# Graph kernel with four layers: the last batch's gate products and layer 3 rows move from GpSimd to VectorE, and the order of all work is planned again

## The chip, the cores and the metric

The kernel runs on one core of a Trainium2 chip. The metric is the device time of one execution in microseconds, taken as the median of several runs. The core has five engines that work side by side, each on its own queue of instructions: TensorE (PE in the profile), VectorE (DVE), ScalarE (ACT), GpSimd (POOL) and SyncE (SP), which here only issues DMAs.

## The reference

There are 16 graphs (batches 0 to 15) of 1024 nodes with 128 features, each with a weighted adjacency matrix of 1024 x 1024 in float32. Four layers follow one another; each takes h = relu(layernorm(x)) and adds its result to x:

```
layer 0, three times:  h = h W + b;  nh = h / |h|;  h = (adj * (nh nh^T)) h      (relu after the first two)
layer 1:  y = relu(((1+eps) h + adj^T h) W1 + b1) W2 + b2, masked by node
layer 2:  softmax(where(adj > 0, tanh(s1_i + s2_j), -1e15)) (h W)
layer 3:  h' = x W^T + b;  e = h' (A + A^T) h'^T;  att = softmax(where(adj > 0, e, 0), axis=1) * adj
          hp = relu(att h')
          i, f, o = sigmoid(gate_k([x, hp]))       (three gates, one number per node each)
          result = o * tanh(sigmoid(i * hp + f * x))
```

In layer 3, x stands for the layer's normalized input. The three gates scale whole rows of 128 features by one number per node. These scalings, and the product with adj in the attention, are what the change moves.

## The kernel before, in words

A batch lies in SBUF as [128 partitions, 8 blocks x 128 features]; node c*128 + p is block c of partition p. The 1024 x 1024 matrices are worked through in eight rows of blocks (index j), each in two halves of 512 columns (HALVES)[...]. Matrices of the form S S^T are symmetric: class Square computes only the blocks on and above the diagonal (L753) and fills in the others by transposing kept blocks (kept by ScalarE at L785, transposed by TensorE at L763). In batches 1 to 13 one quarter of the mirrored blocks goes by VectorE (L775) and a round trip through HBM instead.

Layer 3 (`layer3`) has for each row j: the mask (L1169, VectorE, two halves), the maximum of the row (L1181, VectorE), exp with the row's sum (L1185, ScalarE), the product with adj (L1194, VectorE, two halves), the reciprocal of the sum (L1199) and the scaling of h' by it (L1203, ScalarE), then two accumulating matmuls (`accumulate`, L815). In the last two batches every second row's product with adj is one instruction on GpSimd instead (L1190). After the loop come the eviction of the sums (L615), a small projection psN (L593), its eviction hp (L1216) and `finish`.

`finish(lo, hi)` computes the gates (L1237 VectorE, L1261 ScalarE, L1262 VectorE), z = f * hn on GpSimd (L1265), z = i * hp + z, two Tanh (L1241, L1242), z = o * z + x, and issues the output's DMA on ScalarE's queue (L1272). The two multiply-add steps are in `scaled`. For most batches it is eight VectorE instructions, one for each block of 128 features (L1255). For batches 14 and 15 (`late`) it is one product and one sum on GpSimd (L1248, L1249) for the whole range. Batch 15 calls finish twice, for blocks 0 to 3 and 4 to 7; every other batch calls it once for all eight blocks.

Nothing is issued in the order in which it is written. Every step is recorded as an Op with its engine, an assumed duration and the buffers that it reads and writes. `Plan.order` then plays all of them through once, when the kernel is built: it takes the engine that can start earliest, and among that engine's ready steps the one with the smallest rank. A step's rank is its batch's deadline, less the assumed time of what still hangs on it, less its lead:

```
lead = self.leads.get(o.key + o.edge, self.leads.get(o.key, 0.0))
o.rank = (self.deadline(o.batch) - o.tail - lead, o.seq)
```

Deadlines are 60 apart (PERIOD), the last batch's only LAST behind that of the one before. LEADS is a table of numbers by layer, engine and tile, with own entries for the first two batches (<0, <1) and the last two (>1 for batch 14, >0 for batch 15). POOLS gives the number of buffers of each sort; KINDS gives, by use, the sort, the most that may be held, and the most for a batch that is not the oldest. A larger lead makes a step go earlier. Steps with the flag `port` on VectorE, and all of GpSimd, exclude one another in the plan. The order that comes out is the order of each engine's queue on the chip.

Of the kernel before, what the change touches and what calls it, by code (L numbers as in the profile page):

```python
# [8 lines left out]
F32 = mybir.dt.float32  # L9
# [3 lines left out]
AX = mybir.AxisListType  # L13
# [209 lines left out]
def tile_adj_preln(  # L223
# [66 lines left out]

    R = B * NB
# [22 lines left out]
    eye3 = const.tile([D, E3], F32, name="eye3")  # L314
    load_const(third, b3e[:, 0:D], L3_W_b.partition_broadcast(P))
    for g, (w, v) in enumerate(((L3_ig_w, L3_ig_b), (L3_fg_w, L3_fg_b), (L3_og_w, L3_og_b))):
        at = slice(D + g, D + g + 1)
        load_const(third, w3e[:, at], w[0, 0:D].rearrange("(p o) -> p o", o=1))
        load_const(third, eye3[:, at], w[0, D : 2 * D].rearrange("(p o) -> p o", o=1))
        load_const(third, b3e[:, at], v.partition_broadcast(P))  # L320
    for load_it in first:
        load_it()
# [10 lines left out]
    POOLS = {"adjT": 16, "adjL": 5, "x": 3, "big": 13, "above": 2, "got": 1, "bank": 8, "small": 29, "row": 8, "hbm": 3, "hrow": 2}  # L333
    KINDS = {
        "adjT": ("adjT", 16, 16), "adjL": ("adjL", 5, 5), "x": ("x", 3, 3), "w4": ("big", 10, 6),
        "chunk": ("big", 12, 4), "above": ("above", 2, 1), "got": ("got", 1, 1), "ps": ("bank", 8, 8),
        "acc": ("bank", 8, 8), "small": ("small", 7, 6), "row": ("row", 4, 2), "hbm": ("hbm", 3, 2),
        "hrow": ("hrow", 2, 1),
    }
    PERIOD, LAST, AHEAD, WINDOW = 60.0, 9.0, 2, 0.05  # L340

    LEADS = {
        "0 ACT hT": 10, "0 ACT hn": -27, "0 DVE hn": -7.5, "0 DVE mv": 18.5, "0 DVE nb": -2, "0 DVE st": -7,
        "0 PE ps": 6, "0 POOL rstd": -23, "00 ACT above": -218, "00 ACT hT": 68.5, "00 ACT hTn": -53.5,
        "00 ACT sq": -48, "00 DMA by": 63.5, "00 DMA got": -27.5, "00 DVE above": -233, "00 DVE ew": -9,
        "00 DVE h": -18.5, "00 DVE ss": -111, "00 PE acc0": -166.5, "00 PE ps": -134, "00 PE psP": -26,
        "01 ACT above": 3.5, "01 ACT hT": 55, "01 ACT hTn": -8.5, "01 ACT sq": 54.5, "01 DMA by": -23,
        "01 DMA got": 26, "01 DVE above": 4, "01 DVE ew": 108.5, "01 DVE h": -56, "01 DVE ss": 126.5,
        "01 PE acc0": -136, "01 PE ps": 9, "01 PE psP": -303.5, "02 ACT above": 5, "02 ACT hTn": -115.5,
        "02 ACT sq": 6.5, "02 DMA by": 38, "02 DMA got": -41, "02 DVE above": -10.5, "02 DVE ew": -116,  # L350
        "02 DVE h": -5, "02 DVE ss": -17, "02 DVE x": -78, "02 PE acc0": -116, "02 PE ps": -15, "02 PE psP": 12,
        "02 PE sq": 175, "02 POOL rn": 47.5, "1 ACT g": -36, "1 ACT hn": -48.5, "1 ACT y1": -1.5,
        "1 DMA adjL": -41.5, "1 DVE adjL": -57, "1 DVE hn": -11.5, "1 DVE mv": -94, "1 DVE nb": 152,
        "1 DVE st": -539.5, "1 DVE x": 119.5, "1 PE acc1": -1, "1 PE py": -157, "1 PE py2": -10.5,
        "1 POOL rstd": -12, "2 ACT e2": -4, "2 ACT h": 114.5, "2 ACT hfl": -3.5, "2 ACT hn": -82,
        "2 ACT hnT": -9, "2 DVE alone": 5, "2 DVE e2": 105, "2 DVE h": -2.5, "2 DVE hn": 2.5,
        "2 DVE hrow": -74.5, "2 DVE mv": 11.5, "2 DVE nb": 36.5, "2 DVE rden": 26.5, "2 DVE st": -3,
        "2 DVE x": -11, "2 PE acc2": 5.5, "2 PE p1": 1.5, "2 PE pf": 22, "2 PE ps": 23.5, "2 PE psP": -299.5,
        "2 POOL rstd": 4.5, "3 ACT above": 93, "3 ACT e3": 29, "3 ACT gT": 13.5, "3 ACT gate": -70,
        "3 ACT h3T": -6, "3 ACT hn": 9, "3 ACT hnT": 66.5, "3 ACT hp": -371, "3 ACT hs": -94, "3 ACT z": -137,  # L360
        "3 DMA by": -47.5, "3 DMA got": 34.5, "3 DMA z": -167.5, "3 DVE above": 23.5, "3 DVE e3": -253.5,
        "3 DVE gate": -473.5, "3 DVE h": -119, "3 DVE hn": -0.5, "3 DVE mv": -27.5, "3 DVE nb": 25,
        "3 DVE st": -150, "3 DVE top": -14, "3 DVE z": -942, "3 PE acc3": -134, "3 PE pg": -81, "3 PE ps": 54,
        "3 PE psN": -465.5, "3 PE psP": 3.5, "3 PE sq": 73, "3 POOL rstd": -109.5, "3 POOL z": -13.5,
        "T ACT adjT": -44, "T DMA adjT": 10.5, "T DVE adjT": -411.5, "0 ACT hT <0": -20.5, "0 ACT hT <1": 6,
        "0 ACT hT >0": 6, "0 ACT hT >1": 12, "0 ACT hn <0": -3, "0 ACT hn <1": 49, "0 ACT hn >0": 0,
        "0 ACT hn >1": 31, "0 DVE hn <0": -146.5, "0 DVE hn <1": -18, "0 DVE hn >0": -50, "0 DVE hn >1": 34,
        "0 DVE mv <0": -8.5, "0 DVE mv <1": 29.5, "0 DVE mv >0": 4, "0 DVE mv >1": -11, "0 DVE nb <0": 27,
        "0 DVE nb <1": -61, "0 DVE nb >0": -16.5, "0 DVE nb >1": 51.5, "0 DVE st <1": -11.5, "0 PE ps <0": 25.5,
        "0 PE ps <1": 4, "0 PE ps >0": 9, "0 PE ps >1": 22, "0 POOL rstd <0": 35, "0 POOL rstd <1": 12.5,  # L370
        "0 POOL rstd >0": -77, "0 POOL rstd >1": -19.5, "00 ACT above <0": -4, "00 ACT above <1": -60,
        "00 ACT above >0": -198.5, "00 ACT above >1": -41.5, "00 ACT hT <0": 1.5, "00 ACT hT <1": 11,
        "00 ACT hT >0": 21.5, "00 ACT hT >1": -18, "00 ACT hTn <0": -28.5, "00 ACT hTn <1": 60.5,
        "00 ACT hTn >0": -127, "00 ACT hTn >1": -97.5, "00 ACT params <0": -7.5, "00 ACT sq <0": 223,
        "00 ACT sq <1": 321.5, "00 ACT sq >0": -46, "00 ACT sq >1": 179.5, "00 DMA by <1": 0.5,
        "00 DMA got <1": -76, "00 DMA params <0": 12, "00 DVE above <1": -159, "00 DVE ew <0": 0,
        "00 DVE ew <1": -57.5, "00 DVE ew >0": -155, "00 DVE ew >1": -235.5, "00 DVE h <0": -3,
        "00 DVE h <1": -148.5, "00 DVE h >0": 45, "00 DVE h >1": -2.5, "00 DVE params <0": 60,
        "00 DVE ss <0": 109, "00 DVE ss <1": 12.5, "00 DVE ss >0": -8.5, "00 DVE ss >1": -228.5,
        "00 PE acc0 <0": -64, "00 PE acc0 <1": -216.5, "00 PE acc0 >0": -246, "00 PE acc0 >1": -266.5,  # L380
        "00 PE params <0": 101, "00 PE ps <0": 0, "00 PE ps <1": -36.5, "00 PE ps >0": 39, "00 PE ps >1": -91.5,
        "00 PE psP <0": 20, "00 PE psP <1": -2, "00 PE psP >0": 47, "00 PE psP >1": -187.5, "00 PE sq <1": 51,
        "00 PE sq >0": -4, "00 PE sq >1": 3, "01 ACT above <0": 49.5, "01 ACT above <1": -68.5,
        "01 ACT above >0": -16, "01 ACT above >1": 0, "01 ACT hT <0": 8, "01 ACT hT <1": -76.5,
        "01 ACT hT >0": 21, "01 ACT hT >1": -53.5, "01 ACT hTn <0": 15, "01 ACT hTn <1": -21,
        "01 ACT hTn >0": 10, "01 ACT hTn >1": 0, "01 ACT sq <0": 29, "01 ACT sq <1": 86, "01 ACT sq >0": -54,
        "01 ACT sq >1": 6.5, "01 DMA by <1": 0, "01 DMA got <1": 29, "01 DVE above <1": 0, "01 DVE ew <0": 24,
        "01 DVE ew <1": 57, "01 DVE ew >0": 205.5, "01 DVE ew >1": -87, "01 DVE h <0": -89.5,
        "01 DVE h <1": -30.5, "01 DVE h >0": -5, "01 DVE h >1": 0, "01 DVE ss <0": 29, "01 DVE ss <1": 29.5,
        "01 DVE ss >0": 45, "01 DVE ss >1": -13, "01 PE acc0 <0": 0, "01 PE acc0 <1": -39.5,  # L390
        "01 PE acc0 >0": -2, "01 PE acc0 >1": 3, "01 PE ps <1": 9.5, "01 PE ps >0": 6, "01 PE psP <0": 11,
        "01 PE psP <1": -150.5, "01 PE psP >0": -16.5, "01 PE psP >1": -73, "01 PE sq <0": 67,
        "01 PE sq <1": -4, "01 PE sq >0": 5, "01 PE sq >1": 4.5, "01 POOL rn <0": -3.5, "01 POOL rn <1": -3.5,
        "01 POOL rn >0": -3.5, "01 POOL rn >1": -3.5, "02 ACT above <0": 20, "02 ACT above <1": 23,
        "02 ACT above >0": 30, "02 ACT above >1": -7, "02 ACT hTn <0": -14.5, "02 ACT hTn <1": 48,
        "02 ACT hTn >0": -16, "02 ACT hTn >1": 45.5, "02 ACT sq <0": 37, "02 ACT sq <1": -112,
        "02 ACT sq >0": 0.5, "02 ACT sq >1": 67.5, "02 DMA by <1": 23, "02 DMA got <1": -100,
        "02 DVE above <1": 0, "02 DVE ew <0": -27, "02 DVE ew <1": -155.5, "02 DVE ew >0": -74.5,
        "02 DVE ew >1": -196, "02 DVE h <0": 1.5, "02 DVE h <1": -37, "02 DVE h >0": -20.5,
        "02 DVE h >1": -32.5, "02 DVE ss <0": -12.5, "02 DVE x <0": -108, "02 DVE x <1": -32,  # L400
# [993 lines left out]
```

## Time and profile before

| | us |
|---|---|
| median of three runs | 2461.91 (2461.11 to 2462.0) |
| the profiled execution | 2464.46 |
| span of its profile | 2462.7 |
| TensorE busy | 2397.5 |
| VectorE busy | 2106.1 |
| ScalarE busy | 1291.5 |
| GpSimd busy | 254.5 |
| L1190, eight on GpSimd | 20.1 |
| L1194, 240 half rows on VectorE | 157.2 |
| L1255, 224 multiply-adds on VectorE | 61.1 |

The times of the profile belong to the one profiled execution. Busy time of one engine overlaps with that of others, so the sums say little on their own; what counts is which engine works while TensorE does not. A line of a stretch gives its bounds in us from the start of the span, its length, and for each engine the busy time and, behind the x, the number of instructions that began in it; PEclk is the granted clock of TensorE, DMA the busy share of the DMA engines. A matmul of float32 stands in the trace as two records.

### The profile page before, as it was taken

Reading aid. Unit: us, or ns where it says so; the run is one execution under the profiler, and the core shown is the slowest. Engines: PE = TensorE matmul, PEld = TensorE weight load, DVE = VectorE, ACT = ScalarE, POOL = GpSimd, SP = SyncE. Lnnn points to the kernel's source line nnn. Section 1 sums busy time; section 2 is a strip of 40 time slices with the busy share of each in tenths; the row PEclk is TensorE's granted clock in tenths of the full one; section 3 lists DMA queues with packets and bytes.
Section 4 is the critical chain, followed back from the end, with each engine's and each line's share of the span. In section 5 each row is a group of like instructions: output and inputs, shape, how many; then the busy total and the mean of one; then the engine's idle time right before and its main releaser. Section 6 shows DMA issues by size and latency. Waiting matters only on the chain.

```text
span 2462.7 us, 34845 instructions
## 1 busy us (share of the span) xinstructions
PE 2397.5 (97%) x11946; PEld 1592.9 (65%) x11946; DVE 2106.1 (86%) x5232; ACT 1291.5 (52%) x2404; POOL 254.5 (10%) x155
## 2 busy tenths in 40 slices
PE   6999999999999999999999999999999999999985
PEld 3568576775756657576675766657576675765763
DVE  6758889888998989899898998989899898897585
ACT  4415564735546465464644646465464745656274
POOL 1001010100101101010010101101010010100025
PEclk9999999999999999999999999999999999999998
DMA  8731929658394764928649394774929646072000
GB/s 132 125 103 35 167 56 144 139 89 160 72 159 112 107 142 94 174 67 147 136 82 167 65 164 114 100 145 93 173 73 146 134 86 133 28 96 75 26 1 18
DMA packets 1129473, 263.35 MB, mean 107 GB/s; under 512 B 971856, under 2 KB 1112912, under 8 KB 1129296
## 3 DMA queue, kind: packets, MB, share of 16 engines
q1 hardware_dynamic: 1108368, 251.73, 57.3%
q10 hardware_dynamic: 20928, 9.40, 1.4%
q8 instruction: 94, 1.54, 0.3%
q14 instruction: 83, 0.68, 0.1%
HBM read 198.14 MB, written 62.91 MB: 106 GB/s over the span
## 4 chain that ended last, share of the span: by engine, by line
PE 86%; DVE 5%; DMA 4%; ACT 3%; SPq 1%; POOL 1%; issue 0%; POOLq 0%; DVEq 0%; ACTq 0%
PE acc L815 33%; PE sq L753 17%; PE acc L826 17%; PE psP L593 6%; PE sq L763 4%; PE py L1014 2%; PE py L603 2%; PE ps_hTn L562 2%; DMA adjT<-in_adj_dram 1%; DMA by_hbm<-above 1%; PE ps_hnT L562 1%; PE pg L603 1%; DVE ew L952 1%; PE psN L593 1%; SPq L872 1%; DMA got<-by_hbm 1%
## 5 line engine op out<-in xcount | busy, mean ns | idle before, releaser
L952 DVE SCALAR_TENSOR_TENSOR ew<-sq,rn,adjT 128x512 f32<-128x512 f32 x612 | 437.9, 741 | 92.8 <-ACT above L785 33.0
L815 PE MATMUL acc<-ew,h 128*128 128x512 f32 x1024 | 488.0, 598 | 8.6 <-DVE ew L952 8.3
L753 PE MATMUL sq<-hTn 128*128 128x512 f32 (+3 forms) x1152 | 432.3, 488 | 0.4 <-ACT hTn L615 0.3
L785 ACT COPY above<-sq 128x384 f32<-128x384 f32 (+3 forms) x432 | 167.6, 392 | 431.8 <-PE sq L763 257.4
L753 PEld LDWEIGHTS sq<-hTn 128*128 128x128 f32 x1152 | 198.8, 191 | 152.6 <-issue 104.3
L815 PEld LDWEIGHTS acc<-ew,h 128*128 128x128 f32 x1024 | 177.7, 191 | 164.8 <-issue 120.9
L555 POOL TENSOR_TENSOR rstd<-ve,mhalf 128x8 f32<-128x8 f32 x64 | 107.5, 1679 | 1572.5 <-DVE ve L674 1524.3
L826 PEld LDWEIGHTS acc<-h,ew 128*128 128x128 f32 x2048 | 243.1, 192 | 29.9 <-issue 17.3
L826 PEld LDWEIGHTS acc<-h,e 128*128 128x128 f32 x2048 | 240.5, 194 | 25.6 <-issue 13.3
L826 PE MATMUL acc<-h,ew 128*128 128x128 f32 x2048 | 252.3, 276 | 0.9 <-DVE ew L952 0.9
L826 PE MATMUL acc<-h,e 128*128 128x129 f32 x2048 | 243.1, 277 | 3.4 <-DVE e L1102 3.4
L815 PE MATMUL acc<-e,hs 128*128 128x512 f32 x512 | 242.1, 595 | 0.5 <-DVE e L1194 0.5
L883 ACT ACTIVATE adjT<-adjT 128x1024 f32<-128x1024 f32 x128 | 135.2, 1057 | 203.8 <-DVE adjT L880 136.2
L815 PE MATMUL acc<-adjL,hn 128*128 128x512 f32 x512 | 229.6, 593 | 0.1
L763 PEld LDWEIGHTS sq<-ident,above 128*128 128x128 f32 x960 | 125.2, 141 | 122.1 <-issue 79.2
L1185 ACT ACTIVATE e<-e,top 128x1024 f32<-128x1024 f32 x128 | 146.8, 1147 | 105.3 <-DVE top L1181 103.6
L763 PE MATMUL sq<-ident,above 128*128 128x128 f32 x960 | 175.5, 274 | 5.5 <-ACT above L785 5.4
L1102 DVE SCALAR_TENSOR_TENSOR e<-adjT,e 128x512 f32<-128x512 f32 x256 | 161.5, 685 | 14.6 <-ACT e L1098 14.4
L880 DVE STREAM_TRANSPOSE adjT<-adjT 128x1024 f32<-128x1024 f32 x128 | 154.5, 1223 | 14.5 <-DMA adjT<-in_adj_dram 13.9
L775 DVE STREAM_TRANSPOSE above<-sq 128x512 f32<-128x512 f32 x208 | 147.3, 709 | 21.6 <-PE sq L753 19.6
L815 PEld LDWEIGHTS acc<-adjL,hn 128*128 128x128 f32 x512 | 93.9, 190 | 102.8 <-issue 88.1
L1194 DVE TENSOR_TENSOR e<-e,adjT 128x512 f32<-128x512 f32 x240 | 157.2, 686 | 0.0
(129 smaller groups left out, 3534.2 us busy)
## 6 DMA issues: line engine op xcount, KB each, us to landing
adjT<-in_adj_dram SPq DMA_DIRECT2D x512, 128.0 KB, 4.2
adjL<-in_adj_dram SPq DMA_DIRECT2D x128, 512.0 KB, 5.0
by_hbm<-above SPq DMA_DIRECT2D x104, 512.0 KB, 4.1
got<-by_hbm SPq DMA_DIRECT2D x416, 128.0 KB, 3.9
x<-in_x_dram SPq DMA_DIRECT2D x15, 512.0 KB, 5.4
out_dram<-z ACTq DMA_DIRECT2D x15, 512.0 KB, 5.9
x<-in_x_dram SPq DMA_DIRECT2D x2, 256.0 KB, 4.4
out_dram<-z ACTq DMA_DIRECT2D x2, 256.0 KB, 2.3
```

The source lines that it names most:

```text
L593: nc.tensor.matmul(dst.t[:, (c - lo) * n : (c - lo + 1) * n], cols(srcT.t, c), w, start=True, stop=True)
L753: lambda: nc.tensor.matmul(dst.t[:, (first - lo) * P :], cols(leftT.t, j), span(rightT.t, first, hi), start=True, stop=True),
L763: nc.tensor.transpose(cols(dst.t, r), cols(above.t, p), ident)
L775: lambda: nc.vector.transpose(span(above.t, p, p + 4), read.t),
L785: lambda: nc.scalar.copy(span(above.t, p, p + hi - first), read.t[:, (first - lo) * P :]),
L815: lambda s=s, lo=lo, hi=hi: nc.tensor.matmul(acc[s].t, cols(h.t, at, w), span(ew.t, lo, hi), start=(j == 0), stop=(j == NB - 1)),
L826: nc.tensor.matmul(a.t[:, (c - lo) * n : (c - lo + 1) * n], cols(ew.t, c), h.t[:, j * w : j * w + n], start=(j == 0 and c == lo), stop=(j ...
L880: dve(V(N), [t], [t], lambda t=t: nc.vector.transpose(t.t, t.t), True)
L952: lambda view=view, ew=ew, rn=rn, j=j, lo=lo, hi=hi: nc.vector.scalar_tensor_tensor(by_block(span(ew.t, lo, hi), D, 4), view(), rn.t[:, j ...
L1102: lambda e=e, j=j, lo=lo, hi=hi: nc.vector.scalar_tensor_tensor(span(e.t, lo, hi), span(aT[j].t, lo, hi), 0.0, span(e.t, lo, hi), op0=ALU. ...
L1185: lambda e=e, top=top, tot=tot: nc.scalar.activation(e.t[:, 0:N], e.t[:, 0:N], AF.Exp, bias=top.t, accum_out=tot.t),
L1194: lambda e=e, j=j, lo=lo, hi=hi: nc.vector.tensor_mul(span(e.t, lo, hi), span(e.t, lo, hi), span(aT[j].t, lo, hi)),
```

## The change

It has four parts. A new flag T makes batch 15 `final`: its scalings by the gates become VectorE instructions, block by block, and its layer 3 rows stay on VectorE. Batch 14 keeps what it had on GpSimd. The durations that the plan assumes for some GpSimd steps are raised. The plan's settings are new: buffers, limits, LAST, and the table of leads (559 entries before, 551 after). The rest prepares variants under flags that are not set (E, u, v), and gives `accumulate_nodes` a further argument.

```diff
-    POOLS = {"adjT": 16, "adjL": 5, "x": 3, "big": 13, "above": 2, "got": 1, "bank": 8, "small": 29, "row": 8, "hbm": 3, "hrow": 2}
+    POOLS = {"adjT": 16, "adjL": 5, "x": 3, "big": 13, "above": 2, "got": 1, "bank": 8, "small": 29, "row": 6, "hbm": 3, "hrow": 2}
     KINDS = {
-        "adjT": ("adjT", 16, 16), "adjL": ("adjL", 5, 5), "x": ("x", 3, 3), "w4": ("big", 10, 6),
-        "chunk": ("big", 12, 4), "above": ("above", 2, 1), "got": ("got", 1, 1), "ps": ("bank", 8, 8),
-        "acc": ("bank", 8, 8), "small": ("small", 7, 6), "row": ("row", 4, 2), "hbm": ("hbm", 3, 2),
+        "adjT": ("adjT", 16, 16), "adjL": ("adjL", 5, 5), "x": ("x", 3, 3), "w4": ("big", 12, 8),
+        "chunk": ("big", 11, 4), "above": ("above", 2, 1), "got": ("got", 1, 1), "ps": ("bank", 5, 5),
+        "acc": ("bank", 8, 6), "small": ("small", 7, 6), "row": ("row", 3, 3), "hbm": ("hbm", 3, 2),
         "hrow": ("hrow", 2, 1),
     }
-    PERIOD, LAST, AHEAD, WINDOW = 60.0, 9.0, 2, 0.05
+    PERIOD, LAST, AHEAD, WINDOW = 60.0, 52.0, 2, 0.05
...
-    FLAGS = set("Cabcdkxhyz")
+    FLAGS = set("CabcdkxhyzT")
...
+    def far(b, product):
+
+        return (b > 0 or "v" in FLAGS and product > 0) and b < (B - 1 if "u" in FLAGS else B - 2)
...
-            square = Square(k, hTn, hTn, "abc"[i] in FLAGS and LO <= b < B - HI)
+            square = Square(k, hTn, hTn, "abc"[i] in FLAGS and far(b, i))
...
-            if ("5" in FLAGS or "z" in FLAGS and b >= B - 2) and j % 2:
-                pool_op(1.96, [e, aT[j]], [e], lambda e=e, j=j: nc.gpsimd.tensor_mul(e.t[:, 0:N], e.t[:, 0:N], aT[j].t))
-            for lo, hi in () if ("5" in FLAGS or "z" in FLAGS and b >= B - 2) and j % 2 else HALVES:
+            if ("5" in FLAGS or "z" in FLAGS and (b == B - 2 if "T" in FLAGS else b >= B - 2)) and j % 2:
+                pool_op(2.45, [e, aT[j]], [e], lambda e=e, j=j: nc.gpsimd.tensor_mul(e.t[:, 0:N], e.t[:, 0:N], aT[j].t))
+            for lo, hi in () if ("5" in FLAGS or "z" in FLAGS and (b == B - 2 if "T" in FLAGS else b >= B - 2)) and j % 2 else HALVES:
...
-        late = b >= B - 2
+        late = b == B - 2 if "T" in FLAGS else b >= B - 2
+        final = "T" in FLAGS and b == B - 1
...
-                if "P" in FLAGS or ("y" in FLAGS and late):
+                if not final and ("P" in FLAGS or ("y" in FLAGS and late)):
                     us = 0.2 + 1.7 * n / NB
                     pool_op(us, [blk(a, lo, hi, w), at], [blk(a, lo, hi, w)], lambda: nc.gpsimd.tensor_mul(part(a, w), part(a, w), per_node(of(g), n)))
-                    pool_op(us, [blk(a, lo, hi, w), blk(c, lo, hi)], [blk(z, lo, hi)], lambda: nc.gpsimd.tensor_add(part(z), part(a, w), part(c)))
+                    pool_op(us + 0.4 * n / NB, [blk(a, lo, hi, w), blk(c, lo, hi)], [blk(z, lo, hi)], lambda: nc.gpsimd.tensor_add(part(z), part(a, w), part(c)))
                     return
...
-            pool_op(
-                0.2 + 1.7 * n / NB, [blk(hn, lo, hi), at], [blk(z, lo, hi)],
-                lambda: nc.gpsimd.tensor_mul(part(z), part(hn), per_node(of(1), n)),
-            )
+            if final:
+
+                def of_x():
+                    for k in range(lo, hi):
+                        nc.vector.tensor_scalar_mul(cols(z.t, k), cols(hn.t, k), gate.t[:, 3 * k + 1 : 3 * k + 2])
+
+                dve(n * 0.17, [blk(hn, lo, hi), at], [blk(z, lo, hi)], of_x)
+            else:
+                pool_op(
+                    0.2 + 1.7 * n / NB, [blk(hn, lo, hi), at], [blk(z, lo, hi)],
+                    lambda: nc.gpsimd.tensor_mul(part(z), part(hn), per_node(of(1), n)),
+                )
```

## The prediction

> **What bounds the kernel now.** I read the page's busy shares first, then busy time by stretch, then the chain of work and the timeline at the end. All working below is in times of the profiled execution: a span of 2462.7 us, reported as 2464.46 us, where the three unprofiled runs have a median of 2461.91 us. I take the change of the span off the median.
>
> ```profile
> PE 2397.5 (97%) x11946; PEld 1592.9 (65%) x11946; DVE 2106.1 (86%) x5232; ACT 1291.5 (52%) x2404; POOL 254.5 (10%) x155
> ```
>
> TensorE is busy for all but 65.2 us. The change leaves its matmuls as they are, so all that can be won lies in those 65.2 us. Where are they?
>
> ```profile
> core 0: us, PE busy (x) PEld busy (x) DVE busy (x) ACT busy (x) POOL busy (x), PEclk, DMA share, GB/s
> 0.00:60.00 60.00, 39.52 (x153) 22.94 (x154) 37.29 (x104) 26.20 (x51) 8.92 (x11) 0.94 0.89 131
> 60.00:2340.00 2280.00, 2270.45 (x11362) 1510.32 (x11362) 1986.43 (x4944) 1192.62 (x2221) 201.17 (x119) 1.00 0.61 112
> 2340.00:2400.00 60.00, 50.48 (x299) 39.28 (x298) 49.59 (x133) 43.37 (x75) 11.31 (x6) 0.91 0.00 1
> 2400.00:2437.00 37.00, 37.00 (x139) 20.36 (x137) 29.35 (x49) 23.66 (x51) 12.17 (x6) 1.00 0.00 1
> 2437.00:2462.70 25.70, 0.03 (x1) 0.00 (x0) 3.46 (x4) 5.67 (x10) 20.94 (x15) 0.55 0.14 41
> ```
>
> Length less TensorE's busy time gives 20.5 us idle at the start, 9.5 in the whole middle, 9.5 where the last two batches share layers 2 and 3, none to 2437, and 25.7 after the last matmul. In that tail only GpSimd works, 20.94 of 25.7 us. The chain and the timeline say on what:
>
> ```profile
> 2440.78 2.16 POOL z L1249
> 2442.94 2.01 POOL z L1265 x2
> 2444.94 1.01 POOL hp L1248
> ...
> 2454.13 1.86 POOL z L1248
> 2455.99 0.04 issue
> 2456.04 2.37 POOLq L1390
> ```
>
> ```profile
> 2436.91 1.91 POOL L1248 TENSOR_TENSOR hp<-hp,gate 128x1024 f32<-128x1024 f32 x1 [4.15 <-DVE gate L1262]
> 2437.14 1.79 DVE L1237 TENSOR_TENSOR gate<-hp,h 128x12 f32<-128x12 f32 x2 [0.37 <-ACT hp L1216]
> ...
> 2451.75 1.04 POOL L1248 TENSOR_TENSOR z<-z,gate 128x512 f32<-128x512 f32 x1
> 2451.82 7.00 ACTq L1272 DMA_DIRECT2D out_dram<-z  x3
> ...
> 2456.07 2.34 POOL L1249 TENSOR_TENSOR z<-z,x 128x1024 f32<-128x1024 f32 x1
> ```
>
> Only batch 15 is finished in halves, so 128x512 is batch 15 and 128x1024 is batch 14. Both end at once, in one GpSimd queue, batch 15's halves ahead of batch 14's last product and sum. After GpSimd stops at 2458.4 come 3.2 us to the landing of 512 KB (2.3 us for a half) and 1.1 us to the end of the span.
>
> **The change part by part.** *Batch 15's gate work leaves GpSimd.* Two halves, each with three products of 1.04 us (L1248 twice, L1265) and sums of 1.17 and 1.26 us (L1249), are 5.55 us, 11.1 in all. In their place VectorE does per half four scalings of 128x128 and two times four multiply-adds. The nearest rows: the eight chained L637 multiply-adds take 2.10 us in the chain, 0.26 each; L691's two-scalar scaling has 73.1 us of busy time for 256, 0.286 each, and I use 0.28 for all. That is 3.4 us per half, 6.7 in all, against 11.1.
>
> The new tail follows from these. The last hp eviction ends at about 2437.1. The gate (L1237, L1261, L1262) took 1.04 us for batch 14, and I take 0.9. By then VectorE is working through the first half; 16 instructions for both halves from about 2437.7 end at 2442.2. The two Tanh of the second half are 0.63 + 0.72 us, so 2443.6; four multiply-adds, 2444.7; 0.1 to the issue, 2.3 to the landing, 1.1 to the end: 2448.2. The tail is 14.5 us shorter, if batch 14 is out of the way.
>
> If batch 14 still ends beside it, its own five GpSimd jobs stay. From 2436.91 the first three end at 2442.9, Tanh (1.06 + 1.15) at 2445.2, product and sum (1.90 + 2.34) at 2449.5, and 4.3 to the end gives 2453.8: 8.9 us shorter. Here the Trainium skill (SBUF — State Buffer, summary for kernel authors) bears on it: a VectorE operation with two SBUF inputs and a GpSimd one that reads SBUF lock each other out for the whole instruction. The row agrees (L1237 on 128x12 under GpSimd's work: 0.93 us each, while 128x24 took 0.18), and its use here is that batch 15's multiply-adds could each wait up to 2.3 us. VectorE's chain has 5.6 us in hand against 2453.8, so two such waits are free and a third is not.
>
> *Batch 15's four GpSimd rows of layer 3 (L1190).* Each was 2.50 us on GpSimd; on VectorE a row is 1.27 us (L1194, two halves), so 5.1 us more for VectorE. Who waits: exp of later rows, and through them the accumulation. The skill (Perfetto Trace Analysis, "Optimizing Scalar/DVE Operations") speaks against it: when VectorE is saturated, give work to others, even to GpSimd, though it adds that the shared port may undo it. By that rule, with VectorE at 18.91 of 20 us in 2380 to 2400, the full 5.1 us land on the path. By the rows less does: from 2400 to 2437 TensorE is full and VectorE has 7.6 us free, and the port costs VectorE time already. The four hn scalings at 2386.25 took 3.15 us beside an L1190, where 1.15 is usual, and a half row 1.04 instead of 0.69: 2.4 us lost over eight rows, so 1.2 back for four. Bounds: -1.2 (only the blocking ends) to +5.1. I take +1.3, nearer the row of the full TensorE, since the last rows fall there.
>
> *What emits the same.* The rewritten test for which squares go by DMA gives batches 1 to 13 as before; the branches under flag E are off; the new argument of the node accumulation changes no address. The wider GpSimd costs only steer the planner. All cost nothing in themselves.
>
> *The new order.* 551 leads replace 559, with one value in common; batch 15's deadline goes from 9 to 52 behind batch 14's; small-projection banks are capped at 5, "row" buffers shrink from 8 to 6, chunk slots change by one. It moves every engine's instructions and the loads on SP's queue. No row of the trace shows it, so I bound it by idle time. Start: 11.9 us pass before the first transpose, so at most 20.5 - 11.9 = 8.6 can be won, and as much lost. Middle: 9.5 us over 2280, so I allow -4 to +5. The stretch 2340 to 2400 is where a choice matters:
>
> ```profile
> 2280.00:2340.00 60.00, 60.00 (x381) 46.70 (x380) 30.25 (x104) 14.93 (x30) 4.91 (x3) 1.00 0.08 27
> ```
>
> VectorE idles half of 2280 to 2340 while batch 14's layer 3 is held back, and is full soon after. A later batch 15 lets batch 14's layer 3 fill that hole: up to -9.5. Its price is a last layer 3 that runs alone. A row costs VectorE 1.27 + 1.2 + 1.27 + 0.07 = 3.8 us (L1169, L1181, L1194, L1199), so 30 for eight; TensorE needs for it 36 blocks by 0.215, 28 transposes by 0.11 and 16 accumulations by 0.86 = 24.6 us (the chain has L815 x2 at 0.86, L763 x4 at 0.44). The difference of 5.4 is idle time, unless TensorE has the other batch's work to do. I count it whole, plus 6 for a layernorm with less beside it, less the 9.5: +2. Sum: -14.5 + 1.3 + 2 = -11.2, and 2461.9 - 11.2 = 2450.7, say 2451.
>
> **The rivals.** *Two batches still end together.* -8.9 + 1.3 = -7.6: 2454. For it: they do now. Against it: the later deadline, and that GpSimd's queue is half as long.
>
> *The new order also repacks start and middle.* Taking half of what is open, -4 and -2, and the stretch even instead of +2: 2443. For it: 20.5 us of start and the hole at 2280. Against it: the start waits on batch 0's adjacency (12.4 us of TensorE in 20 at a DMA share of 0.92), which no order speeds up.
>
> *Slower: batch 15 runs alone from its layer 1.* Mechanism: TensorE has nothing to put beside latency chains. Layer 1 begins with statistics 1.5, aggregation 0.7, power 1.7 and scaling 1.6 = 5.5 us. Layer 2 has the same and then transposed eviction 0.6, projection copy 0.5, score 0.6, Tanh 1.1, Exp 1.0, mask 0.7 = 10, and its loop is bound by ScalarE (eight rows of 1.04 + 0.96 = 16.0 us against 14.3 of TensorE, twice the chain's 7.14 for L826 x64): 1.7. Layer 3 begins with about 9.5, and its loop has 5.4. That is 32 us of idle TensorE instead of 9.5: +22.6 - 14.5 + 1.3 = +9.4, 2471; alone from layer 2 on only, 2466. It decides when idle time before the last matmul grows by more than 14.5 - 1.3 = 13 us, from some 23 us on; at 28 the kernel is slower by 0.2%. For it: the deadline moves by 43 us, and TensorE's clock already falls to 0.91 in this stretch. Against it: deadlines are only a part of the rank, beside leads of hundreds.
>
> **How the numbers follow.** About 0.2% (5 us) is what a measurement of this kernel tells from no change. Forecast 2451: 0.44 (own range 2445 to 2458). Together: 2454, 0.16. Repacked: 2443, 0.2. Alone: 2471, 0.13. The rest, 0.07: all 5.1 us of the rows on the path and a worse start, 2460. Faster (below 2457): nearly all of the first three, 0.76. Slower (over 2467): most of the alone case, 0.11. Same, with the cases of 2460 and 2466 in it: 0.13. The range runs from inside the repacked case to inside the alone case, 2437 to 2465.
>
> **What would show it.** Right: no 128x512 work on GpSimd at the end; four L1190 instead of eight; last matmul to end of span about 11 us instead of 25.7; batch 14's output issued well before batch 15's; TensorE idle for 9 to 13 us in the 100 us before the last matmul. Wrong: batch 14's 128x1024 jobs still last on GpSimd (rival one); idle at the start under 15 us (rival two); over 23 us idle between layer 2 of the last batch and the last matmul (the slower rival).

## The result and the profile after

The changed kernel takes 2441.24 us (median of four runs, 2438.53 to 2441.81) against 2461.51 us before: a ratio of 0.9915, 95% interval 0.9898 to 0.9933, 20.3 us less. The prediction was 2451, in a range of 2437 to 2465. Its direction and its range held; the gain is nearly twice the one forecast, and much of it came from a place where the prediction had counted nothing.

The busy times of the page after, and busy time by stretch (columns as in the table of before; the lines of the new tail are cut at the last matmul):

```profile
PE 2389.2 (98%) x11946; PEld 1588.9 (65%) x11946; DVE 2106.2 (86%) x5264; ACT 1288.3 (53%) x2404; POOL 230.9 (9%) x141
```

```profile
0.00:60.00 60.00, 39.29 (x155) 23.49 (x156) 34.85 (x89) 24.94 (x49) 7.29 (x10) 0.94 0.81 127
60.00:2340.00 2280.00, 2271.82 (x11410) 1515.18 (x11409) 1991.54 (x4992) 1196.65 (x2234) 201.70 (x121) 1.00 0.58 112
2340.00:2400.00 60.00, 55.13 (x310) 38.72 (x308) 48.45 (x115) 47.94 (x85) 21.88 (x10) 1.00 0.00 1
2400.00:2429.20 29.20, 22.79 (x75) 11.46 (x75) 24.88 (x43) 15.10 (x32) 0.00 (x0) 0.94 0.06 18
2429.20:2440.00 10.80, 0.22 (x3) 0.03 (x1) 6.48 (x28) 3.67 (x8) 0.00 (x0) 0.71 0.16 49
```

The tail after the last matmul is 10.8 us instead of 25.7 (10.9 and 25.9 from the start of the last matmul record, as counted below), and GpSimd does nothing in it. Batch 14's gates now stand in GpSimd's queue well ahead of it; the timeline shows the first and the last of its five jobs and the issue of the output:

```profile
2386.91 1.91 POOL L1307 TENSOR_TENSOR z<-hn,gate 128x1024 f32<-128x1024 f32 x1 [1.45 <-PE ps_hnT L570]
...
2397.60 2.37 POOL L1283 TENSOR_TENSOR z<-z,x 128x1024 f32<-128x1024 f32 x1
2400.00 0.38 ACTq L1314 DMA_DIRECT2D out_dram<-z  x1
```

Batch 15's gates follow the last matmul on VectorE; the lines show the first half's scalings and the last multiply-adds of the second half:

```profile
2430.19 0.87 DVE L1301 TENSOR_SCALAR z<-hn,gate 128x128 f32<-128x128 f32 x4
...
2435.48 1.14 DVE L1289 SCALAR_TENSOR_TENSOR z<-z,gate,x 128x128 f32<-128x128 f32 x4 [0.40 <-ACT z L1276]
```

One thing in the page does not fit the reading of before: TensorE has the same 11946 records, but is busy for 8.3 us less. The matmuls are the same, and the clock explains little: before the last matmul it was granted half speed for 20.5 us in the trace of before and for 17.1 us in this one, which is worth 1.7 us at most. So the busy time of before must have held waiting. Two readings show it. The first is the undisturbed middle of both kernels, 400 to 2000 us. Before:

```profile
400.00:2000.00 1600.00, 1595.24 (x7903) 1054.06 (x7903) 1444.02 (x3610) 858.29 (x1593) 148.95 (x88) 1.00 0.68 121
```

After:

```profile
400.00:2000.00 1600.00, 1597.44 (x7951) 1058.97 (x7950) 1449.31 (x3622) 859.27 (x1601) 147.00 (x88) 1.00 0.65 122
```

Busy shares are within 2.2 us of each other, but the second one did 48 more matmul records in the same 1600 us, 0.6%, which is 9.7 us of time. (By the matmul pf, of which every batch has one, ten batches took 466.1 to 1944.1 us before and 469.7 to 1941.3 after: 147.80 and 147.16 each, so 6.4 us less for the ten.) The granted clock was 1.00 in both.

The second reading is of the starts of the records. The distance from one record to the next is nearly always the same for its width: 429 ns for 512 columns, 322 for 384, 215 for 256, 110 to 112 for 128 to 131. What goes beyond it is a stall, whether or not the modelled end covers it. The usual distances sum to 2362.3 us in both kernels; the rest is:

| us | before | after | change |
|---|---|---|---|
| to the first matmul | 11.9 | 12.9 | +1.0 |
| stalls to 100 us | 17.9 | 20.5 | +2.6 |
| stalls 100 to 2200 | 28.6 | 15.4 | -13.2 |
| stalls 2200 to 2340 | 0.7 | 0.9 | +0.2 |
| stalls from 2340 on | 15.4 | 17.1 | +1.7 |
| start of the last record to the end of the span | 25.9 | 10.9 | -15.0 |
| sum | | | -22.7 |

The spans are 2462.7 and 2440.0, so the table closes. Two rows carry the result: the tail, and 13 us of small stalls in the middle. In the middle two single events about cancel: up to 2 us of the stalls of before lie at 238.1 to 241.3 us, where the granted clock was 0.50 (b_both below has that order too, but not this stretch), and the trace of after has one stall of 1.95 us at 751.8, where VectorE had waited 3.11 us for blocks that came back through HBM, which no other trace of the new order shows. One of the small stalls, as it stood in the timeline of before:

```profile
617.38 1.07 ACT L1241 ACTIVATE z<-z 128x1024 f32<-128x1024 f32 x1
618.48 1.15 ACT L1242 ACTIVATE z<-z,half 128x1024 f32<-128x1024 f32 x1
619.53 0.46 ACT L785 COPY above<-sq 128x384 f32<-128x384 f32 x1
...
620.05 0.33 PE L763 MATMUL sq<-ident,above 128*128 128x128 f32 x1 [0.35 <-ACT above L785]
```

ScalarE worked on two gate Tanh of one batch when TensorE needed the copy of blocks for the squares of the next; the copy came late, and TensorE started its record 0.51 us behind the usual distance. The same stall of 0.51 us came back at 768.9, 917.0, 1065.2, 1213.1 and 1361.8, once a batch, ten times up to 1953. In the changed kernel the corresponding record is 0.07 us late, without those two Tanh directly ahead of the copy:

```profile
620.84 0.46 ACT L793 COPY above<-sq 128x384 f32<-128x384 f32 x1
...
621.35 0.33 PE L771 MATMUL sq<-ident,above 128*128 128x128 f32 x1
```

This accounts for 4.4 of the 13 us. The rest is spread over many smaller stalls, most of them at accumulations and projections, whose causes were not followed.

### The profile page after: what moved, and what is told of

Same layout as the page of the kernel before. It is cut to its first block, busy times and chain, and to the rows that moved or that the text cites. A ratio compares the mean times of both kernels' runs of the same rounds, so it can differ in the third digit from the quotient of the medians.

```text
span 2440.0 us, 34840 instructions
## 1 busy us (share of the span) xinstructions
PE 2389.2 (98%) x11946; PEld 1588.9 (65%) x11946; DVE 2106.2 (86%) x5264; ACT 1288.3 (53%) x2404; POOL 230.9 (9%) x141
## 5 line engine op out<-in xcount | busy, mean ns | idle before, releaser
L960 DVE SCALAR_TENSOR_TENSOR ew<-sq,rn,adjT 128x512 f32<-128x512 f32 x612 | 432.0, 738 | 72.1 <-ACT above L793 37.4
L823 PE MATMUL acc<-ew,h 128*128 128x512 f32 x1024 | 481.5, 597 | 3.6 <-DVE ew L960 3.6
L793 ACT COPY above<-sq 128x256 f32<-128x256 f32 (+3 forms) x432 | 167.8, 393 | 439.0 <-PE sq L761 239.7
L834 PEld LDWEIGHTS acc<-h,e 128*128 128x128 f32 x2048 | 232.9, 192 | 11.9 <-issue 6.5
L834 PE MATMUL acc<-h,e 128*128 128x129 f32 x2048 | 233.8, 275 | 1.2 <-DVE e L1110 1.2
L706 ACT ACTIVATE hn<-x,nb,rstd 128x128 f32<-128x128 f32 x256 | 105.3, 483 | 123.6 <-DVE nb L690 117.8
```

The lines of the kernel that those rows point to most:

```text
L793: lambda: nc.scalar.copy(span(above.t, p, p + hi - first), read.t[:, (first - lo) * P :]),
L823: lambda s=s, lo=lo, hi=hi: nc.tensor.matmul(acc[s].t, cols(h.t, at, w), span(ew.t, lo, hi), start=(j == 0), stop=(j == NB - 1)),
L834: nc.tensor.matmul(a.t[:, (c - lo) * n : (c - lo + 1) * n], cols(ew.t, c), h.t[:, at * w : at * w + n], start=(j == 0 and c == lo), stop=( ...
L960: lambda view=view, ew=ew, rn=rn, j=j, lo=lo, hi=hi: nc.vector.scalar_tensor_tensor(by_block(span(ew.t, lo, hi), D, 4), view(), rn.t[:, j ...
```

## The experiments

The theory now: two independent gains, a shorter tail (the gates' engine and batch 14's earlier end share it) and a smoother middle that only the leads made. The rivals: the engine's move alone; the new limits on buffers; the deadline of 52. To move an engine without moving anything else, six kernels keep a plan exactly as it was and only let the function of a planned step issue to the other engine, at the same place of the order.

**Before's order, batch 15's work on VectorE.** `b_gates` (its product of x, L1265, goes to VectorE in the same way):

```diff
-                    pool_op(us, [...], [...], lambda: nc.gpsimd.tensor_mul(part(a, w), part(a, w), per_node(of(g), n)))
-                    pool_op(us, [...], [...], lambda: nc.gpsimd.tensor_add(part(z), part(a, w), part(c)))
+                    pool_op(us, [...], [...], lambda: None if b == B - 1 else nc.gpsimd.tensor_mul(part(a, w), part(a, w), per_node(of(g), n)))
+                    pool_op(us, [...], [...], by_vector if b == B - 1 else lambda: nc.gpsimd.tensor_add(part(z), part(a, w), part(c)))
...
```

> The order of all work is that of the kernel before; only the gate products of batch 15 are issued to VectorE at the places where they stood in GpSimd's queue. Theory 'two parts' (the move of the gates shortens the end, the new order does the rest): batch 14's five GpSimd jobs stay last, so the end comes at about 2453.8 of the span, 8.9 us sooner: 2452 to 2454. Theory 'order alone' (the new order does it all, the engine of the gates hardly counts): 2460 to 2462.

`b_rows` does the same with the product of the odd rows; `row_product` issues two halves to VectorE in batch 15:

```diff
-                pool_op(1.96, [e, aT[j]], [e], lambda e=e, j=j: nc.gpsimd.tensor_mul(e.t[:, 0:N], e.t[:, 0:N], aT[j].t))
+                pool_op(1.96, [e, aT[j]], [e], row_product)
```

> The order of the kernel before; only the four layer 3 rows of batch 15 are multiplied on VectorE. 'Two parts': VectorE has 5.1 us more work where TensorE is mostly full, so +1 to +3: 2462 to 2465. Rival 'saturated' (VectorE sets the pace where the last two batches share it): +5: 2467. Third: the shared port was the cost, so -1 or less: 2460 or below.

`b_both` has both.

> The order of the kernel before with both moves of batch 15. 'Two parts': -8.9 + 1.3, 2454. 'Order alone': 2461 or more. If 'saturated' holds: 2458.

Measured: b_gates 2457.99 (ratio 0.9983, 0.9974 to 0.9992), b_rows 2464.71 (1.0009, 1.0001 to 1.0017), b_both 2459.53 (0.9989, 0.9982 to 0.9997), before on the same chip 2462.03. The two moves alone are worth 2.5 us of the 20. The gates' tail is 20.9 us in both kernels that have them on VectorE, so 5.0 shorter, where 8.9 was expected. The timeline of b_gates says why (L1254, L1255 and L1267, L1252 are its lines for the GpSimd and the VectorE work):

```profile
2439.28 2.17 POOL L1255 TENSOR_TENSOR z<-hp,z 128x1024 f32<-128x1024 f32 x1
2439.34 3.56 DVE L1267 TENSOR_SCALAR z<-hn,gate 128x128 f32<-128x128 f32 x8
...
2443.86 2.90 POOL L1254 TENSOR_TENSOR z<-z,gate 128x1024 f32<-128x1024 f32 x1 [2.41 <-ACT z L1242]
...
2445.40 5.50 DVE L1252 SCALAR_TENSOR_TENSOR z<-z,gate,x 128x128 f32<-128x128 f32 x8 [0.40 <-ACT z L1242]
2446.84 2.34 POOL L1255 TENSOR_TENSOR z<-z,x 128x1024 f32<-128x1024 f32 x1
2449.89 2.04 ACTq L1282 DMA_DIRECT2D out_dram<-z  x3
```

Batch 14's jobs and batch 15's lock each other out: eight multiply-adds take 5.50 us, where the changed kernel has four in 1.14, and GpSimd's product takes 2.90 instead of 1.91. The missing 3.9 us can be placed: batch 14's chain on GpSimd, from 2435.41 to 2449.18, is 1.2 us longer than the 12.6 expected; its output stands in ScalarE's queue behind both halves of batch 15, which VectorE finished at 2450.9, and so was issued 2.3 us after GpSimd was done; and from that issue to the end it took 4.7 us instead of 4.3. The rows cost 2 to 3 us of stalls from 2340 us on: 17.5 in b_rows and 17.6 in b_both, against 15.4 before and 14.2 in b_gates.

**The new order, batch 15's work on GpSimd.** `a_both`, `a_gates` and `a_rows` undo the same in the changed kernel; in a_gates `emit` issues a product and a sum to GpSimd and `of_x` one product, in a_rows the odd rows of batch 15 are one GpSimd instruction in the place of the first half:

```diff
                 def emit():
+                    if final:
+                        nc.gpsimd.tensor_mul(part(a, w), part(a, w), per_node(of(g), n))
+                        nc.gpsimd.tensor_add(part(z), part(a, w), part(c))
+                        return
...
```

> The order of the changed kernel, with batch 15's gates and its four odd layer 3 rows issued to GpSimd at the same places. 'Two parts': with batch 14 out of the way, GpSimd needs 11.1 us for the gates from 2430, so the end comes 5 us later; VectorE is relieved of 5.1 us in a stretch where it is full and TensorE idles some 8 us, which gives back 2 to 4: 2442 to 2445. 'Order alone': the same, within 2 us of the changed kernel. If the move itself were the main thing: above 2450.

> The order of the changed kernel, its rows on VectorE, only batch 15's gates issued to GpSimd. 'Saturated at the end': no help for VectorE, and a tail that is 5 us longer: 2446. If the gates' engine does not count once batch 14 is out of the way: 2441.

> The order of the changed kernel, batch 15's gates on VectorE, its four odd layer 3 rows issued to GpSimd at the same places. 'Saturated at the end' (VectorE alone sets the pace of the last layer 3, so each row costs its whole 1.27 us there): the last matmul comes 5 us sooner than in the changed kernel and the end with it, about 2436, faster than both kernels. 'Hidden' (my +1.3): 2440. 'Port' (the two engines lock each other out): no gain or a loss, 2441 to 2443.

Measured: a_both 2442.44 (0.9916, 0.9902 to 0.9929), a_gates 2443.53 (0.9923, 0.9911 to 0.9936), a_rows 2438.17 (0.9903, 0.9890 to 0.9917). With everything of batch 15 back on GpSimd, nearly all of the gain remains. That is what I had expected of a_both, though the rival 'order alone' expected nearly the same, so it only rules out that the move is the main thing. The gates cost in the tail what was worked out: 15.8 us in both kernels against 10.9. In the medians, a_gates lies 5.4 us above a_rows of the same set. For a_gates, the stretch behind the last matmul:

```profile
2424.30:2439.90 15.60, 0.19 (x2) 0.00 (x0) 1.51 (x4) 3.63 (x8) 10.92 (x10) 0.65 0.11 34
```

GpSimd's ten jobs, 10.92 us, are alone on the path. The rows did not behave as any theory said. In the medians a_rows was 3.1 us below the changed kernel, but these were measured at different times, and its stalls from 2340 us on were not smaller. So it was run again beside the unaltered kernel, with a third kernel that takes batch 14's four odd rows to VectorE too (`a_rows14`).

> The changed kernel unaltered, beside the others of this set on one chip: 2439 to 2443. Its end should read as before: last matmul to end of span 10.9 us.

> The same kernel as the earlier one with batch 15's four odd rows back on GpSimd, again. In the two earlier traces the stalls of TensorE from 2340 us on were 17.1 us with these rows on VectorE and 18.1 on GpSimd, so 'the rows do not matter there': within 1.5 us of the unaltered kernel. If the earlier difference of 3.1 us of the medians is real: 3 us below it.

> The order of the changed kernel, with batch 14's four odd rows issued to VectorE too. They lie at 2340 to 2380, where VectorE is busy for 37.9 of 40 us. 'Saturated': 5.1 us more work there, of which the following idle time of VectorE (10.6 of 20 us busy in 2380 to 2400) takes some: +2 to +5. 'The rows do not matter anywhere': within 1.5 us of the unaltered kernel.

Measured: a_again 2438.34 (0.9900, 0.9886 to 0.9913), a_rows2 2438.37 (0.9900, 0.9887 to 0.9914), a_rows14 2441.45 (0.9915, 0.9902 to 0.9929). The changed kernel itself moved by 2.9 us between its two measurements (2441.24 and 2438.34), so the 3.1 us were not real, and a_rows is no better version. Stalls from 2340 us on are 17.1, 15.6 and 17.0 us in the three traces that have batch 15's rows on VectorE in the new order, and 18.1, 17.8 and 18.5 in the three that have them on GpSimd: about 1.6 us for VectorE, too little for the medians to show. Nor is it clear that the engine made them: the three on GpSimd all have a granted clock of 0.91 in 2380 to 2400, where the changed kernel has 1.00 in both of its traces, and one such stretch of 3.4 us at half speed is worth up to 1.7 us. 'Saturated at the end' fell: taking 5.1 us of work from a full VectorE brought no earlier end; why not was not followed. Batch 14's rows are another matter: 20.4 us of stalls, and 3.1 us more time than a_again of the same set, whose four times are all below the four of a_rows14. They lie where VectorE has no room, in a_rows14:

```profile
2340.00:2360.00 20.00, 16.57 (x74) 10.81 (x73) 20.00 (x34) 15.04 (x27) 0.00 (x0) 0.91 0.00 1
2360.00:2380.00 20.00, 20.00 (x131) 15.84 (x130) 18.66 (x43) 14.90 (x21) 0.00 (x0) 1.00 0.00 1
```

In the first of these a_again, with a VectorE just as full, has TensorE busy for 18.50 us at a granted clock of 1.00. Part of the extra stalls is thus time at a lower clock.

**Planned anew with one setting back.** `a_last9` has LAST at 9, `a_leads` the table of leads of before, `a_buffers` POOLS and KINDS of before; each is otherwise the changed kernel.

```diff
-    PERIOD, LAST, AHEAD, WINDOW = 60.0, 52.0, 2, 0.05
+    PERIOD, LAST, AHEAD, WINDOW = 60.0, 9.0, 2, 0.05
```

> The changed kernel with batch 15's deadline 9 instead of 52 behind batch 14's, and nothing else; the order differs only in the last 13% of TensorE's queue. 'The later deadline takes batch 14 out of the end': both batches end together again, batch 14's GpSimd work in the tail, 2448 to 2453. 'The order of the middle is what counts' (small stalls between matmuls): the middle is the same, so within 4 us of the changed kernel.

> The changed kernel with the leads of before, and nothing else: the new buffers and limits and the deadline of 52 remain. If the new limits (five banks for small projections above all) are what removed the small stalls of the middle, the middle keeps its gain, and the time stays below 2455. If the leads did it, the middle goes back to the 29 us of stalls of before or more: 2455 to 2475, since these leads were not made for these buffers.

> The changed kernel with the buffers and limits of before, and the new leads. If the leads alone smoothed the middle, the stalls of TensorE between 400 and 2000 us stay at about 10 us (18.8 before, 22 with the old leads on the new buffers), whatever happens at the end. If it takes leads and limits together, they go to 18 or more. The time: 2441 if the limits never bind, 2450 to 2500 if they do, as these leads were made for other limits.

Measured: a_last9 2460.00 (0.9990, 0.9984 to 0.9997), a_leads 2508.67 (1.0186, 1.0172 to 1.0200), a_buffers 2461.01 (0.9992, 0.9984 to 1.0000). The times say that every one of the three settings is needed with the other two. a_last9 and a_leads came out slower than any of the expectations had it. The rows of stalls say for what (us, from the trace of each, as in the table above):

| kernel | records in 400 to 2000 | stalls 400 to 2000 | 2200 to 2340 | from 2340 | tail |
|---|---|---|---|---|---|
| before | 7903 | 18.8 | 0.7 | 15.4 | 25.9 |
| b_both | 7898 | 18.9 | 0.7 | 17.6 | 20.9 |
| a_leads | 7899 | 22.2 | 30.8 | 36.5 | 10.9 |
| after | 7951 | 10.1 | 0.9 | 17.1 | 10.9 |
| a_again | 7964 | 6.7 | 2.4 | 15.6 | 10.8 |
| a_both | 7971 | 7.0 | 2.4 | 18.5 | 15.8 |
| a_last9 | 7969 | 6.3 | 12.5 | 17.1 | 21.0 |
| a_buffers | 7956 | 8.5 | 10.2 | 28.6 | 10.8 |

Every kernel with the new leads has the smooth middle, with the old buffers as well; none with the old leads has it, on the new buffers either. In a_leads the stall of 0.51 us is back, once a batch. Its middle, and that of a_buffers:

```profile
400.00:2000.00 1600.00, 1592.20 (x7899) 1052.60 (x7899) 1440.32 (x3603) 855.73 (x1589) 146.61 (x86) 1.00 0.66 121
400.00:2000.00 1600.00, 1598.05 (x7956) 1059.98 (x7956) 1450.72 (x3622) 859.90 (x1602) 147.00 (x88) 1.00 0.66 122
```

So the leads made the middle, and the rivals of the limits and of the deadline fall. One thing is not separated: the raised durations of GpSimd steps are in all kernels with the new leads. Alone they do nothing (a_leads has them too); whether the leads need them was not tried. The deadline of 52 acts at the end only: with 9 the middle stays, but batch 14 comes last again and its five GpSimd jobs fill the tail, which is 10.1 us longer, and 12.5 us of stalls come up at 2200 to 2340. In the tail of a_last9:

```profile
2438.39 1.91 POOL L1307 TENSOR_TENSOR z<-hn,gate 128x1024 f32<-128x1024 f32 x1 [41.99 <-DVE gate L1296]
...
2448.79 2.34 POOL L1283 TENSOR_TENSOR z<-z,x 128x1024 f32<-128x1024 f32 x1
2451.16 0.38 ACTq L1314 DMA_DIRECT2D out_dram<-z  x1
```

The old limits, too, cost only at the end: 10.2 and 28.6 us of stalls there. Which of the limits binds was not tried.

## Why the prediction was right, and where it was not

- **The tail, -14.5: right.** It was -15.0. It divides into -10.1 for batch 14's earlier end (25.9 before, 15.8 in a_both) and -4.9 for the gates' engine (15.8 to 10.9). Taken in the other sequence it is the same: -5.0 for the engine (25.9 to 20.9 in b_gates), then -10.0. The sign named for it, TensorE idle for 9 to 13 us in the 100 us before the last matmul, came out at 11.7. The sum was worked out with 0.28 us for a scaling; four of L1301 took 0.87, so 0.22 each.
- **The case in which both batches end together, -8.9: too much.** b_gates gives -5.0. The lock of VectorE and GpSimd was named there with two waits of up to 2.3 us taken as free; b_gates had five, two in gate steps, one in a scaling and two in multiply-adds, and GpSimd lost time by it too. That batch 14's output would wait in ScalarE's queue for batch 15's was not counted. The rule of the Trainium skill that was cited (SBUF — State Buffer, summary for kernel authors) held, in both directions. The 0.93 us that the prediction read for each of two L1237 is a mean of one that was blocked (1.70 us) and one that was not (0.16).
- **The four rows, +1.3: the right way, a little low, for the order of before** (+2 to +3 of stalls), while in the new order they cost nothing that can be measured. The advice of the skill to offload from a saturated VectorE was right for batch 14's rows (+3.1 when taken back to it) and made no difference for batch 15's.
- **The stretch of the last two batches, +2: right in size** (+1.7 of stalls), but not for the reason given, so in part by luck. The hole at 2280 to 2340 was not filled (VectorE is busy for 33.9 of 60 us there, 30.3 before): batch 14's layer 3 runs at 2340 to 2376 as one block, and batch 15's from 2395 on by itself. And the clock hid a part: TensorE stood at half speed for 10.2 us of this stretch before and for 3.4 after, so the waits proper grew by more than 1.7, up to 5 us.
- **"Middle: 9.5 us over 2280, so I allow -4 to +5": this step failed.** It was -13.2, and the central sum had it at nothing. The 9.5 were length less busy time, and TensorE's busy time held about 20 us of stalls besides (28.6 + 0.7 in the table), since the ends of matmuls are modelled. For the same reason it was wrong that all that can be won lies in the 65.2 us in which TensorE is not busy. The bound was taken from a column that cannot show it. The Trainium skill (Trainium Kernel Development and Optimization, Performance Expectations) warns of this: matmul busy time is a bad metric for how close a kernel is to roofline, as matmuls are pipelined. Of what it offers instead, the share of weight loads is 65% on both pages, but read per stretch it does show the change: in 400 to 2000 us they are busy for 1054.06 us before and 1058.97 after, 0.5% more. The starts of the records, or the records done per stretch, show it too, and the starts show where. The term mis-sized is thus the middle, 0 taken and -13 measured, outside its own bounds, and with the start's +3.6 against it it makes up most of the gap between -11 and -20. That the whole still fell into the range is due to the width allowed for other terms.
- **The start: taken at nothing.** Here +3.6, but it goes from 16.9 to 20.5 us of stalls to 100 us between traces of nearly the same plan (the highest, here and in a_rows, have a second stretch at half clock at 65 us), so nothing can be read from one trace of it.

The measured time is nearest to the rival that repacks start and middle (2443), and that is in part luck: its middle came, but with -13 instead of -2, while its -4 at the start and the sign named for it, under 15 us idle at the start, did not (20.7 us).

The slower rival did not come: batch 15's layer 3 does run alone, at VectorE's pace, but layers 1 and 2 still had company.

## What to carry to other kernels

Before bounding what a new order can win, count instead of measuring busy time: instructions done per stretch in the steady part, or start-to-start distances against the usual one, show stalls that a busy share of 99.7% hides. A tail is to be split by whose work it is: here the order, which decides who comes last, was worth 10 us and the engine 5, in either sequence. An estimate for two engines that share work at the end must count every wait of the one on the other, and the queue in which both outputs stand. To separate an order from an engine, leave the plan alone and swap only what the planned steps issue.

## What the runs showed of the hardware that was not expected

VectorE and GpSimd, working on SBUF at the same time, both lost: in b_gates a GpSimd product took 2.90 us instead of 1.91 and eight multiply-adds 5.50 instead of 2.3, two of the eight having waited. And part of the stalls from 2340 us on is TensorE's clock: before, around a wait of 3.4 us that ended at 2358.9, it was granted about half speed (0.77 and 0.55 in 2355 to 2360 and 2360 to 2365), and 32 records of layer 2 took 6.53 us in the chain, where 3.6 is what their usual distance gives. After the change 2340 to 2400 has a granted clock of 1.00, and the half speed comes at 2410 to 2420 instead (0.83); in a_again, the same program, 2340 to 2420 has 1.00 throughout. What sets it off is not shown, so a difference of 2 us between single traces of this stretch says nothing of the order.
